# Two ResNet bottleneck blocks: the 3x3 convolution adds onto ScalarE's copies of the common product, prepares its input three combinations ahead, and forms a fourth combination by four products

## The chip, the cores and the metric

The kernel runs on one core of a Trainium2 chip. The metric is device time in microseconds (us) of one execution; a time given for a kernel is the median of its runs. A core has five engines with queues of their own: TensorE (PE in the profile; its weight loads are PEld), VectorE (DVE), ScalarE (ACT), GpSimd (POOL) and SyncE (SP), which here only issues DMAs. They meet through semaphores. TensorE writes its results to PSUM[...].

## The reference

Two bottleneck blocks in sequence over x of shape (64, 1024, 14, 14), all in fp32. Batch normalization uses the statistics of the batch itself, so each stage ends with sums over all 64 images before the next can begin.

```python
def block(x, w1, b1, g1, be1, w2, b2, g2, be2, w3, b3, g3, be3, residual_scale):
    out = relu(bn(conv(x, w1, b1, 1, 0), g1, be1))      # 1x1, 1024 -> 256
    out = relu(bn(conv(out, w2, b2, 1, 1), g2, be2))    # 3x3,  256 -> 256
    out = bn(conv(out, w3, b3, 1, 0), g3, be3)          # 1x1,  256 -> 1024
    return relu(x + softplus(residual_scale)[0] * out)

y = block(block(x, *L0), *L1)
```

## The kernel before

**Stages.** Channels lie on the 128 partitions, so 256 channels are MS = 2 slots and 1024 are CS = 8. The stages of a block follow each other: the first 1x1 convolution (`Conv1`, by a scheme of seven half-sized products for eight), the 3x3 convolution (`conv2`, L490), the Gram matrix of its output (`gram`, L798), from which the statistics of the last convolution are worked out (`conv3_stats`, L842), and the last 1x1 convolution with the residual. The last stage of block 0 is fused with the first of block 1 (`fused`, L926); block 1 ends in `final` (L900). The output of conv1, y, stays in SBUF for all 64 images, and conv2 overwrites it in place.

**The 3x3 convolution.** It runs over NG = 8 groups g of GI = 8 images. Along the rows it is a Winograd scheme of four output rows from six input rows: six combinations i = 0..5 of input rows (and of filter rows), each of which is then a convolution along a row only. They are handled in pairs, (1, 2), (3, 4), (5, 0) (`pairs`, L492). Combinations 3 and 4 have 24 lines per slot (3 rows for each of 8 images), the others 32. Along a row the columns are kept as seven odd and seven even ones, and the convolution is done with five products of filters and half lines (names at L70: D0, D1D2, D3, D1, D2), or with four for the combinations in FOUR (L67: 3, 4 and 5; names at L71: D0M2, SUM, DIFF, D3M1). One product is four fp32 matmuls, over 2 input slots and 2 output slots, of 224 columns (168 for combinations 3 and 4). Each such matmul leaves two records in the trace.

With five products, the common one (D1D2, of `sums`) belongs to the odd and the even columns alike, while D1 and D3 go to the odd columns and D2 and D0 to the even ones. With four, SUM (of `sums`) and DIFF (of `diffs`) make both halves, one by their difference and one by their sum, and D3M1 and D0M2 (of `v`, differences of neighbouring columns) are added to one half each.

**What makes and uses them.** `combine` (L516) makes the inputs of a pair: row combinations by VectorE (helper `stt`, whose line L514 shows in the profile), then in `ready` (L523) `sums` on VectorE (L531), `diffs` on GpSimd (L534), `v` on VectorE (L538) with its edge columns on ScalarE (L542, L543), and the load of the combination's filters `u` from DRAM on SyncE's queue (L547, three buffers). `products` (L590) issues the matmuls (L606 for the common products, L616 for the columns with four products, L629 for those with five), each result in one of eight PSUM banks with a common tag "ps"; ScalarE then copies the common product to SBUF (`ms`, L657 and L661). `finish` (L685) adds them on VectorE (`shared_part` L669, `column` L677), forms the output rows and writes them to y. The loop at L774 works on one pair while `combine` makes the next. Beside it ScalarE normalizes the y of the next group (`norm`, L480) and takes the moments of the group before last (`moment`, L754), whose activations of 1568 elements are the long pieces of its work.

**Filters.** `filters` (L157) makes the u of one block from the 3x3 filters, quarter by quarter (2 input slots by 2 output slots). For block 0 VectorE does it during conv1. For block 1 GpSimd does it, in four pieces beside `gram` of block 0 (`beside`, L1113: tile step 2 + 12i). A piece uses two buffers of the pool that also holds images (tag "x", four buffers in block 0); `conv3_stats` takes one more for its q (L860), and the image pairs x_0, x_1 are loaded into the same buffers after that.

**Order.** A scheduler orders each engine's instructions by readiness; matmuls that use the helper `matmul` (L155), and instructions given to `tc.keep_in_program_order`, keep their order in the program. PSUM and SBUF tiles come from pools in turn: a tile waits until the last reader of the buffer's previous content is done.

Of the kernel before, what the change touches and what calls it, by code (L numbers as in the profile page):

```python
# [33 lines left out]
FP = mybir.dt.float32  # L35
AF = mybir.ActivationFunctionType
# [26 lines left out]
BUFS = dict(u=3, t=3, r=4, sums=4, diffs=2, v=2, ms=3, f=2)  # L63
# [3 lines left out]
FOUR = 3, 4, 5  # L67
NKS = [4 if i in FOUR else 5 for i in range(NF)]
NK = max(NKS)
D0, D1D2, D3, D1, D2 = range(5)  # L70
D0M2, SUM, DIFF, D3M1 = range(4)  # L71
# [11 lines left out]
def bottlenecks(ctx: ExitStack, tc: tile.TileContext, x, w1s, w2s, w3s, pars, out):  # L83
# [73 lines left out]
    def filters(eng, b, s, o, spare):  # L157
# [24 lines left out]
        for i, (row, more, op, by) in parts.items():  # L182
# [16 lines left out]
            else:  # L199
                scaled(u[:, 0:3, :].rearrange("p k m -> p (k m)"), row, by)  # L200
                eng.tensor_tensor(
                    u[:, D1 : D2 + 1], u[:, D0 : D3 + 1 : D3 - D0], u[:, D1D2 : D1D2 + 1].to_broadcast([P, 2, P]),
                    ALU.subtract,
# [276 lines left out]
    def norm(s, y, aff):  # L480

        scale, shift = aff
        nc.scalar.activation(y, y, AF.Relu, bias=shift[:, s : s + 1], scale=scale[:, s : s + 1])
# [6 lines left out]
    def conv2(psum, pool, b, par, aff, stats):  # L490

        pairs = [(g, p) for g in range(NG) for p in ((1, 2), (3, 4), (NF - 1, 0))]  # L492
# [23 lines left out]
        def combine(g, pair, between=None):  # L516
# [4 lines left out]
            made = []  # L521

            def ready(i, r):  # L523
# [21 lines left out]
                u = pool.tile([P, MS * MS * NK * P], FP, tag="u", name="u", bufs=BUFS["u"])  # L545
                u = u[:, : MS * MS * NKS[i] * P].rearrange("p (s o k m) -> p s o k m", s=MS, o=MS, m=P)
                nc.sync.dma_start(out=u, in_=us[b][i])  # L547
                made.append((i, lines, r, sums, diffs, u))

            both = slice(0, MS)  # L550
            if pair[0] == 1:
# [11 lines left out]
                ready(1, ra)  # L563
                nc.vector.tensor_sub(rb, t1, t2)
                ready(2, rb)
            elif pair[0] == 3:
# [6 lines left out]
                ready(3, ra)  # L573
                stt(rb, t4, -2.0, t3)
                ready(4, rb)
            else:
# [7 lines left out]
                ready(NF - 1, rb)  # L584
                for s in range(MS):
                    stt(ra[:, s, 1:], rows(g, s, 0, 1, RT), 4.0, ra[:, s, 1:])
                ready(0, ra)
            return made

        def products(made, first):  # L590


            done = []
            for i, lines, r, sums, diffs, u in made:
                n = lines * WH
                four = i in FOUR

                def bank():
                    return psum.tile(2 * RT * GI * WH).rearrange("p (o n) -> p o n", o=MS)

                less = bank() if four else None
                m = bank()
                eos = [bank() for o in range(MS)]

                def shared(to, k, v, o, s):
                    nc.tensor.matmul(  # L606
                        to[:, o, :n], u[:, s, o, k], v[:, s].rearrange("p l c -> p (l c)"),
                        start=(s == 0), stop=(s == MS - 1),
                    )

                def columns(o, s, part):

                    odd, even = (eos[o][:, q, :n].rearrange("p (l c) -> p l c", c=WH) for q in range(2))
                    if four:
                        to, k, v = ((odd, D3M1, r[:, s, :, WH:]), (even, D0M2, r[:, s, :, :WH]))[part]
                        nc.tensor.matmul(to, u[:, s, o, k], v, start=(s == 0), stop=(s == MS - 1))  # L616
                        return
                    to, k, v = (
                        (odd, D1, r[:, s, :, WH:]),
                        (odd[:, :, : WH - 1], D3, r[:, s, :, WH + 1 :]),  # L620
                        (even, D2, r[:, s, :, :WH]),
                        (even[:, :, 1:], D0, r[:, s, :, : WH - 1]),
                    )[part]
                    start = s == 0 and part % 2 == 0
                    stop = s == MS - 1 and part % 2 == 1
                    if by_slot:

                        start, stop = s + part == 0, s == MS - 1 and part == 3
                    nc.tensor.matmul(to, u[:, s, o, k], v, start=start, stop=stop, skip_group_check=by_slot)  # L629

                by_slot = first and not done
                each = list(itertools.product(range(MS), range(MS)))
                if four:
                    for to, k, v in ((less, DIFF, diffs), (m, SUM, sums)):
                        for o, s in each:
                            shared(to, k, v, o, s)
                    for o in range(MS):
                        for part in range(2):
                            for s in range(MS):
                                columns(o, s, part)  # L640
                elif by_slot:
                    for s, o in each:
                        for part in range(4):
                            columns(o, s, part)
                    for o, s in each:
                        shared(m, D1D2, sums, o, s)
                else:
                    for o in range(MS):
                        for s in range(MS):
                            shared(m, D1D2, sums, o, s)  # L650
                        for part in range(4):
                            for s in range(MS):
                                columns(o, s, part)
                ms = pool.tile([P, MS, RT * GI * WH], FP, tag="ms", name="ms", bufs=BUFS["ms"])
                if i == 1:
                    for o in range(MS):
                        nc.scalar.activation(  # L657
                            ms[:, o, :n], m[:, o, :n], AF.Identity, bias=par[:, B2 + o : B2 + o + 1]
                        )
                else:  # L660
                    nc.scalar.activation(ms[:, :, :n], (less if four else m)[:, :, :n], AF.Copy)  # L661
                done.append((four, lines, m, ms, eos))
            return done

        def halves(f, lines):

            return f.rearrange("p o r (i q c) -> p o q (r i) c", i=GI, q=2)[:, :, :, :lines]

        def shared_part(item, f):  # L669

            four, lines, m, ms, eos = item
            if four:
                a, l = (v[:, :, : lines * WH].rearrange("p o (l c) -> p o l c", c=WH) for v in (m, ms))
                for q, op in enumerate((ALU.subtract, ALU.add)):
                    nc.vector.tensor_tensor(halves(f, lines)[:, :, q], a, l, op)

        def column(item, f, o):  # L677
            four, lines, m, ms, eos = item
            n = lines * WH
            to = more = halves(f, lines)[:, o]  # L680
            if not four:
                more = ms[:, o, None, :n].to_broadcast([P, 2, n]).rearrange("p q (l c) -> p q l c", c=WH)
            nc.vector.tensor_tensor(to, eos[o][:, :, :n].rearrange("p q (l c) -> p q l c", c=WH), more, ALU.add)

        def finish(g, pair, done, acc):  # L685

            fa, fb = (new("f", full if pair[0] == 3 else RT) for i in range(2))
# [482 lines left out]
```

## Time and profile before

| | |
|---|---|
| median of 3 runs | 2070.32 us (2069.67 to 2071.58) |
| the profiled execution | 2071.47 us, of which the span of its instructions is 2069.7 |
| mean granted TensorE clock | 0.987 |
| conv1 of block 0 ends on TensorE | 314.4 us |
| 3x3 stage of block 0 on TensorE | 321.4 to 618.95 us |
| head of the fused stage, TensorE idle | 745.9 to 752.2 us |
| conv1 of block 1 ends on TensorE | 1340.5 us |
| 3x3 stage of block 1 on TensorE | from 1347.4 us |

How to read it: times are us from the start of the span; engines are as named above, L12 is line 12 of the kernel, and an operand is given as partitions x elements. The page's second part shows forty slices of the span with the busy share of each engine in tenths:

```profile
PE   8999998999998989999999999899999899999998
DVE  6776559999883466777777767699989734799997
ACT  1011116224225035555555555462332330555555
POOL 0100001122218953333343333210322000566665
```

The 3x3 stages are slices 7 to 12 and 27 to 32: TensorE and VectorE are both nearly full there, ScalarE has the least to do. The peak of GpSimd at slices 13 to 15 is the filters of block 1. The largest groups of VectorE, ScalarE and GpSimd in two later groups of the 3x3 stage of block 0 (472 to 546 us) are these; the columns are line, engine, operation, output<-input, shapes, count, then busy us and mean ns of one, then the idle time before them and what ended it:

```profile
L683 DVE TENSOR_TENSOR f<-ps,ms 128x448 f32<-128x448 f32 x12 | 7.4, 616 | 3.3 <-PE ps L629 3.3
L702 DVE TENSOR_TENSOR fa<-f 128x896 f32<-128x896 f32 x2 | 4.1, 2058 | 0.0
L675 DVE TENSOR_TENSOR f<-ps,ms 128x336 f32<-128x336 f32 x8 | 3.6, 494 | 0.0
L755 ACT ACTIVATE idle<-y,center 128x1568 f32<-128x1568 f32 x9 | 14.3, 1591 | 0.0
L661 ACT ACTIVATE ms<-ps 128x448 f32<-128x448 f32 x6 | 3.3, 543 | 31.2 <-PE ps L606 31.2
L534 POOL TENSOR_TENSOR diffs<-r 128x336 f32<-128x336 f32 x5 | 17.6, 3521 | 34.1 <-DVE r L514 34.1
```

### The profile page before, as it was taken

Reading aid. Unit: us, or ns where it says so; the run is one execution under the profiler, and the core shown is the slowest. Engines: PE = TensorE matmul, PEld = TensorE weight load, DVE = VectorE, ACT = ScalarE, POOL = GpSimd, SP = SyncE. Lnnn points to the kernel's source line nnn. Section 1 sums busy time; section 2 is a strip of 40 time slices with the busy share of each in tenths; the row PEclk is TensorE's granted clock in tenths of the full one; section 3 lists DMA queues with packets and bytes.
Section 4 is the critical chain, followed back from the end, with each engine's and each line's share of the span. In section 5 each row is a group of like instructions: output and inputs, shape, how many; then the busy total and the mean of one; then the engine's idle time right before and its main releaser. Section 6 shows DMA issues by size and latency. Waiting matters only on the chain.

```text
span 2069.7 us, 27894 instructions
## 1 busy us (share of the span) xinstructions
PE 2009.1 (97%) x10120; PEld 1709.2 (83%) x10120; DVE 1572.0 (76%) x2946; ACT 809.3 (39%) x1591; POOL 657.5 (32%) x668
## 2 busy tenths in 40 slices
PE   8999998999998989999999999899999899999998
PEld 4555558999998879999999999899999898555554
DVE  6776559999883466777777767699989734799997
ACT  1011116224225035555555555462332330555555
POOL 0100001122218953333343333210322000566665
PEclk9999999999999989999999999999999999999999
DMA  7664425555533244444444444255555420589998
GB/s 285 235 240 162 184 94 191 181 206 184 199 138 125 99 190 160 183 168 176 183 160 187 160 184 172 100 197 197 194 181 206 160 92 20 222 320 339 326 340 300
DMA packets 73338, 395.33 MB, mean 191 GB/s; under 512 B 7024, under 2 KB 38000, under 8 KB 44400
## 3 DMA queue, kind: packets, MB, share of 16 engines
q1 hardware_dynamic: 63168, 324.26, 43.6%
q10 hardware_dynamic: 5904, 51.91, 6.0%
q0 software_dynamic: 4128, 17.37, 2.2%
q8 instruction: 80, 1.31, 0.3%
q14 instruction: 58, 0.48, 0.1%
HBM read 276.60 MB, written 116.92 MB: 190 GB/s over the span
## 4 chain that ended last, share of the span: by engine, by line
PE 80%; DVE 6%; POOL 6%; DMA 4%; issue 3%; ACT 1%; SPq 0%; DVEq 0%; POOLq 0%; ACTq 0%
PE ay L155 13%; PE ps L629 13%; PE cy L155 13%; PE ps L606 9%; PE ap L155 7%; PE cp L155 7%; PE ps L616 6%; PE ax L155 4%; PE cx L155 4%; POOL spare L168 2%; PE cp L810 2%; DMA x<-mid 2%; DVE x L400 2%; PE ps L155 1%; PE ap L811 1%
## 5 line engine op out<-in xcount | busy, mean ns | idle before, releaser
L274 ACT ACTIVATE cu<-cy,scale 128x196 f32<-128x196 f32 (+1 forms) x552 | 257.0, 474 | 305.8 <-PE cy L155 297.4
L534 POOL TENSOR_TENSOR diffs<-r 128x336 f32<-128x336 f32 (+1 forms) x48 | 115.5, 2408 | 651.3 <-DVE r L514 453.9
L629 PE MATMUL ps<-r,u 128*128 128x224 f32 (+1 forms) x1536 | 293.7, 343 | 13.9 <-DVE r L562 7.0
L629 PEld LDWEIGHTS ps<-r,u 128*128 128x128 f32 x1536 | 279.3, 190 | 17.8 <-issue 14.8
L400 DVE SCALAR_TENSOR_TENSOR x<-cp,scale,x 128x196 f32<-128x196 f32 (+1 forms) x368 | 178.0, 484 | 84.4 <-PE cp L155 82.3
L274 ACT ACTIVATE x<-x,shift 128x392 f32<-128x392 f32 x368 | 211.7, 614 | 68.4 <-POOL x L426 52.1
L155 PE MATMUL cy<-ct,w3s 128*128 128x196 f32 (+1 forms) x736 | 222.3, 384 | 2.5 <-ACT cu L274 2.5
L421 POOL TENSOR_TENSOR x<-x,cu 128x196 f32<-128x196 f32 (+1 forms) x184 | 167.7, 912 | 175.6 <-ACT cu L274 167.8
L155 PE MATMUL ay<-at,w1s 128*128 128x196 f32 (+1 forms) x752 | 209.3, 381 | 1.0 <-ACT au L274 1.0
L426 POOL TENSOR_TENSOR x<-x,cu 128x392 f32<-128x392 f32 x124 | 125.9, 1015 | 193.3 <-DVE x L400 188.5
L155 PEld LDWEIGHTS ay<-at,w1s 128*128 128x128 f32 x752 | 136.5, 190 | 35.4 <-ACT au L274 1.9
L155 PEld LDWEIGHTS cy<-ct,w3s 128*128 128x128 f32 x736 | 134.2, 191 | 36.8 <-ACT cu L274 4.0
L606 PE MATMUL ps<-sums,u 128*128 128x224 f32 (+1 forms) x768 | 156.0, 337 | 0.0
L447 POOL TENSOR_TENSOR x<-x,cu 128x392 f32<-128x392 f32 x120 | 125.1, 1042 | 83.4 <-DVE x L400 78.4
L274 ACT ACTIVATE au<-ay 128x196 f32<-128x196 f32 (+1 forms) x141 | 53.7, 381 | 241.7 <-PE ay L155 235.8
L661 ACT ACTIVATE ms<-ps 128x448 f32<-128x448 f32 (+1 forms) x80 | 40.4, 504 | 266.8 <-PE ps L606 266.8
L606 PEld LDWEIGHTS ps<-sums,u 128*128 128x128 f32 x768 | 133.0, 189 | 0.1
L400 DVE SCALAR_TENSOR_TENSOR x<-cx,scale,x 128x196 f32<-128x196 f32 (+1 forms) x184 | 89.1, 484 | 57.0 <-PE cx L155 51.3
L155 PE MATMUL cy<-y,w 128*128 128x196 f32 (+1 forms) x416 | 130.4, 401 | 1.1 <-DVE x L891 1.1
L616 PE MATMUL ps<-v,u 128*128 128x168 f32 (+1 forms) x768 | 131.1, 322 | 0.0
L155 PE MATMUL cx<-y,w 128*128 128x196 f32 (+1 forms) x404 | 125.9, 397 | 0.6 <-DVE x L891 0.6
L616 PEld LDWEIGHTS ps<-v,u 128*128 128x128 f32 x768 | 123.8, 188 | 0.8
(209 smaller groups left out, 4080.3 us busy)
## 6 DMA issues: line engine op xcount, KB each, us to landing
x<-in_x SPq DMA_DIRECT2D x62, 1568.0 KB, 6.6
u<-u SPq DMA_DIRECT2D x48, 1280.0 KB, 5.5
x<-mid SPq DMA_DIRECT2D x32, 1568.0 KB, 9.3
u<-u SPq DMA_DIRECT2D x48, 1024.0 KB, 4.8
mid<-x ACTq DMA_DIRECT2D x31, 1568.0 KB, 5.1
out<-x SPq DMA_DIRECT2D x124, 392.0 KB, 6.6
u<-y POOLq DMA_DIRECT2D x12, 320.0 KB, 5.7
u<-spare POOLq DMA_DIRECT2D x12, 320.0 KB, 2.5
```

The lines of the kernel that those rows point to most:

```text
L155: tc.keep_in_program_order(nc.tensor.matmul(*args, **kw))
L168: eng.tensor_scalar(to, v, by, None, ALU.mult)
L274: tc.keep_in_program_order(nc.scalar.activation(*args, **kw))
L400: nc.vector.scalar_tensor_tensor(v, bank, self.scale[:, o : o + 1], v, ALU.mult, ALU.add)
L421: nc.gpsimd.tensor_add(self.part(1, 1), self.part(1, 1), u3)
L426: nc.gpsimd.tensor_add(v, v, self.u12)
L447: nc.gpsimd.tensor_add(v, v, self.u12[:, i * self.n : (i + 1) * self.n])
L534: nc.gpsimd.tensor_sub(diffs, r[:, :, :, :WH], r[:, :, :, WH:])
L606: nc.tensor.matmul(to[:, o, :n], u[:, s, o, k], v[:, s].rearrange("p l c -> p (l c)"), start=(s == 0), stop=(s == MS - 1),)
L616: nc.tensor.matmul(to, u[:, s, o, k], v, start=(s == 0), stop=(s == MS - 1))
L629: nc.tensor.matmul(to, u[:, s, o, k], v, start=start, stop=stop, skip_group_check=by_slot)
L810: nc.tensor.matmul(g0, zt[:, c, 0:P], zt[:, c, :], start=first, stop=last)
```

## The change

**Products.** Combination 2 joins FOUR, so four of six combinations have four products. The layout of the filters changes with it: the common product's filter comes first, D0 and D3 lie next to each other, and `filters` scales a five-product combination in two instructions (D0 with D3, then D1D2) where it was one.

**Accumulation.** The PSUM banks have tags now: "l", "m", "odd" and "even", two each. A combination's common product goes to bank m, and ScalarE copies it (with the bias, for combination 1) into the combination's own odd and even banks (`start`, `biased`). The matmuls of the columns have no start flag and add to what lies there. With four products, the difference product goes to bank l and by ScalarE to SBUF (`ls`), and VectorE's one addition or subtraction per half gives the output (`outputs`); with five the banks already hold the result, and `finish` reads them straight into its sums. For the very first combination of a stage, `columns` opens the banks with a start flag, and the common product goes through `later` to `ls`. At the start of the stage four matmuls with the identity write all odd and even banks once.

**Order.** Inputs are made by a generator, one combination at a time, three ahead. The matmuls keep their order in the program: for each combination the difference product, then a part of its columns, the common product of the next combination, then the rest of its columns. The long pieces of ScalarE's work (`norm`, `moment`) go through `act`, which keeps them in program order, one after the copies of each combination (`long_work`). The load of u is split into the first product (`ua`) and the rest (`ub`), with three buffers each.

**Around it.** `conv3_stats` takes q from the pool of the Gram matrix's stage (passed as `one`) and not from the images' buffers. The pieces of filters beside `gram` start at tile step 1 + 12i.

```diff
-BUFS = dict(u=3, t=3, r=4, sums=4, diffs=2, v=2, ms=3, f=2)
+BUFS = dict(ua=3, ub=3, t=2, r=4, sums=3, diffs=4, v=3, ls=3, f=2)
-FOUR = 3, 4, 5
+FOUR = 2, 3, 4, 5
-D0, D1D2, D3, D1, D2 = range(5)
-D0M2, SUM, DIFF, D3M1 = range(4)
+D1D2, D0, D3, D1, D2 = range(5)
+SUM, DIFF, D0M2, D3M1 = range(4)
...
-                scaled(u[:, 0:3, :].rearrange("p k m -> p (k m)"), row, by)
+                row = row.rearrange("p (k m) -> p k m", k=3)
+                scaled(u[:, D0 : D3 + 1], row[:, 0::2], by)
+                scaled(u[:, D1D2], row[:, 1], by)
...
+        for tag in COLUMNS * 2:
+            n = MS * RT * GI * WH
+            matmul(psum.tile(n, tag), ident, ident[:, :1].to_broadcast([P, n]), start=True, stop=True)
...
-                u = pool.tile([P, MS * MS * NK * P], FP, tag="u", name="u", bufs=BUFS["u"])
-                nc.sync.dma_start(out=u, in_=us[b][i])
+                for tag, a, e in (("ua", 0, 1), ("ub", 1, NKS[i])):
...
+            def biased(self, to, m):
+                for v in to:
+                    if self.i == 1:
+                        for o in range(MS):
+                            nc.scalar.activation(v[:, o], m[:, o], AF.Identity, bias=par[:, B2 + o : B2 + o + 1])
+                    else:
+                        nc.scalar.activation(v, m, AF.Copy)
+            def later(self, k, v, op):
+                l = self.whole("l", k, v)
+                ls = pool.tile([P, MS * RT * GI * WH], FP, tag="ls", name="ls", bufs=BUFS["ls"])
+                self.ls, self.op = ls[:, : MS * self.n].rearrange("p (o n) -> p o n", o=MS), op
+                self.biased([self.ls], l)
+            def start(self):
+                self.ls = None
+                self.banks = {q: self.bank(COLUMNS[q]) for q in (EVEN, ODD)}
+                if not self.first:
+                    self.biased(self.banks.values(), self.whole("m", 0, self.sums))
+            def middle(self):
+                if self.four:
+                    self.later(DIFF, self.diffs, ALU.subtract)
+            def columns(self, *qs):
...
+                for q, o, (a, e, k, v), s in steps:
+                    to = self.banks[q][:, o].rearrange("p (l c) -> p l c", c=WH)[:, :, a:e]
+                    matmul(
+                        to, self.filter(s, o, k), v[:, s], start=self.first and q not in opened, stop=True,
+                        skip_group_check=True,
+                    )
+                    opened.add(q)
+                if self.first:
+                    self.later(0, self.sums, ALU.add)
...
+        def outputs(c):
+            f = new("f", c.lines // GI)
+            for q in c.banks:
+                c.add(q, half(f, q), c.column(q))
+            return f
...
+                if fa is not None:
+                    nc.vector.tensor_add(a, fa, fb)
+                    nc.vector.tensor_sub(d, fa, fb)
                 else:
+                    for q in ca.banks:
+                        nc.vector.tensor_tensor(half(a, q), ca.column(q), half(fb, q), ALU.add)
+                        nc.vector.tensor_tensor(half(d, q), ca.column(q), half(fb, q), ALU.subtract)
...
+        def long_work(g, k):
+            if g + 1 < NG and k in (1, 2):
+                norm(k - 1, y_grp[:, k - 1, g + 1], aff, act)
+                return
+            i = (0, None, None, 1, 2, 3)[k] if g + 1 < NG else k
+            if g > 1 and i < 4:
+                moment(g - 1, i // 2, i % 2)
...
+        queue = [next(made) for i in range(3)]
+        queue[0].start()
+        for k in range(NG * NF):
+            item, more = queue[0], queue[1:2]
+            item.middle()
+            qs = tuple(item.banks)
+            if item.first:
+                item.columns(*qs)
+                qs = ()
+            elif more and more[0].four:
+                item.columns(qs[0])
+                qs = qs[1:]
+            for v in more:
+                v.start()
+            long_work(*divmod(k, NF))
+            item.columns(*qs)
+            finished.send(item)
+            queue = queue[1:] + list(itertools.islice(made, 1))
...
-        q = pool.tile([P, MS, C], FP, tag="x", name="q")
+        q = one.tile([P, MS, C], FP, tag="q", name="q")
...
-            conv2(Psum(scope, ["ps"], ps=8), pool, b, pb, aff, stats2)
+            conv2(Psum(scope, ["l"], l=2, m=2, odd=2, even=2), pool, b, pb, aff, stats2)
...
-                        beside.update({2 + 12 * i: partial(piece, i // MS, i % MS) for i in range(MS * MS)})
+                        beside.update({1 + 12 * i: partial(piece, i // MS, i % MS) for i in range(MS * MS)})
```

## The prediction

> **What bounds the kernel now.** I read the page first: shares, slices, chain. Then the clock and busy time of the 3x3 stage, its waits and TensorE's timeline over one group; last the two places where TensorE stands still next to it.
>
> ```profile
> PE 2009.1 (97%) x10120; PEld 1709.2 (83%) x10120; DVE 1572.0 (76%) x2946; ACT 809.3 (39%) x1591; POOL 657.5 (32%) x668
> 361.00:398.00 37.00, 37.00 (x218) 36.78 (x217) 37.00 (x73) 5.64 (x15) 3.76 (x2) 1.00 0.54 193
> 509.00:546.00 37.00, 37.00 (x218) 36.78 (x217) 34.33 (x61) 12.15 (x26) 9.11 (x4) 1.00 0.54 193
> PE ps L629 <- DVE r L562: 7.0, 1, 7.0
> PE ps L629 <- DMA u<-u: 6.9, 1, 6.9
> ```
>
> TensorE is busy 97% of the span. The window rows give length, then busy us (instructions) of TensorE, weight loads, VectorE, ScalarE, GpSimd, then clock, DMA share, GB/s. In a group of the 3x3 convolution TensorE is busy for all 37.00 us at full clock, VectorE 37.00 in group 1 and 34.33 later, ScalarE only 12.15. The last two lines are all the waits of TensorE in the 3x3 stages (321 to 619 and 1347 to 1645): one each, at the start. So a matmul removed there is time, if VectorE and ScalarE keep up.
>
> ```profile
> 515.19 0.92 PE L606 MATMUL ps<-sums,u 128*128 128x224 f32 x4
> 515.94 3.02 PE L629 MATMUL ps<-r,u 128*128 128x224 f32 x16
> ...
> 522.41 1.30 PE L606 MATMUL ps<-diffs,u 128*128 128x168 f32 x8
> ...
> 531.61 1.67 PE L606 MATMUL ps<-diffs,u 128*128 128x224 f32 x8
> 533.12 1.68 PE L606 MATMUL ps<-sums,u 128*128 128x224 f32 x8
> 534.64 3.23 PE L616 MATMUL ps<-v,u 128*128 128x224 f32 x16
> 537.70 0.92 PE L606 MATMUL ps<-sums,u 128*128 128x224 f32 x4
> ```
>
> Starts in this timeline price a combination (each matmul leaves two records). Combination 2 with five products runs from 515.19 to 522.41: 7.22 us. Combination 5, also 32 lines but four products, from 531.61 to 537.70: 6.09. One product is 533.12 to 534.64, 1.51.
>
> ```profile
> 321.30:323.00 1.70, 1.63 (x5) 1.58 (x6) 1.60 (x3) 1.70 (x2) 0.00 (x0) 0.50 1.02 433
> 743.20 7.99 DMA x<-in_x
> 752.22 1.02 PE L155 MATMUL cp<-y,w3s 128*128 128x196 f32 x2 [6.01 <-DVE x L400]
> 755.00:758.30 3.30, 3.30 (x12) 3.30 (x12) 1.27 (x3) 1.87 (x5) 0.00 (x0) 0.50 1.01 402
> ```
>
> After each start wait the clock is 0.50 for some us. The other place is the head of the fused stage: the load of image pair 1 starts at 743.20, when GpSimd's last filter piece gives its buffer back, takes 7.99, and TensorE stands 6.01, then runs at half clock from 752.2 to 758.3.
>
> [...]
>
> **The change part by part.**
>
> (1) *Matmuls.* Combination 2 drops a product: 7.22 − 6.09 = 1.13 by these starts. Over the group (the same kind of line comes again after 36.97 us, of which combinations 3 and 4 take 4.60 each by their starts) it is 1.15 with 7.23 and 6.08; I take 1.15, times 8 groups, times 2 blocks: −18.4. In the very first combination of each block the new `columns` is called a second time with an empty tuple, and its last two lines then compute the sums product again: one more product of 1.51, twice, +3.0. It stands on TensorE's path, as nothing else delays it. Together −15.4.
>
> (2) *Additions moved from VectorE to ScalarE and TensorE.* Every combination now has its common product copied by ScalarE into both column banks (twelve copies of 448 or 336 per group), and the four-product ones get a copy of the difference product (four), for six `ms` copies before. By 543 and 450 ns that is ten more copies, some 5.2 us, plus 0.6 for the edge columns of combination 2: ScalarE goes from 12.15 to about 18 of 35.8 us. The share hides it; the question is when each copy is due. TensorE's new order puts the columns of the current combination (and the difference product of the next) between m and the columns that need its copy. The shortest cover is at combination 3's even bank: odd(2) 1.51 + difference product 1.14 = 2.65 us, against a copy of 0.45 that first needs VectorE to have read combination 1's even bank. Queued ahead of a copy on ScalarE can be one activation of 1591 ns (row L755; the normalization is as wide), since one long piece is put after each pair of copies: about 0.5 us of margin there in the worst case, more elsewhere. What waits behind a late copy is TensorE itself. Bounds: 0 to 1.6 per group. I take 0 for the steady groups and +1 for each kernel as a whole, since group 1 has VectorE at 37.00 of 37.00 and its release of banks is late there.
>
> (3) *VectorE per group.* Gone, at the rows of the groups view for two later groups: two adds of 448 in combination 1 (2 x 0.61), four of 336 in 3 and 4 (4 x 0.49), two of 448 in 5 (2 x 0.61), and in 0 four of 448 become four of 224 (−0.9). New: outputs a and d in four pieces of 448 for two of 896 (+0.3), and the edge differences of combination 2 (row of v, 0.94). About −4, from 34.3 to some 30.5 of 35.8. [...] I take no gain (nothing waits on VectorE in the steady groups) and no loss; the loss side is rival 3.
>
> (4) *Inputs three ahead, filter loads split.* The first 1/5 of u comes in 512 B pieces. The stage's DMA share is 0.54, so 48 more issues on SP and shorter pieces hide, except at the start of block 1, where u's load ends the wait: +0.4 (0 to 1).
>
> (5) *Identity matmuls at the start.* Four of 448 columns, two products' worth of the 1.51 above, so 3.0 at full clock and up to 6 at half, in the 7 us wait[...]. That clock cost 0.5 x 1.7 + 0.46 x 2.0 = 1.8 in block 0 and about 2.3 in block 1. −3 (0 to −4), since I do not know how near to the end of the wait they run.
>
> (6) *GpSimd's filters for block 1, and q.* Combination 2 becomes four-product: scaling 1.17 and subtraction 0.73 go, three of 0.46 to 0.53, one of 0.85 and two of 0.58 come: +1.6, and two split scalings add about 0.1 each: +1.8 a piece, +7 for four. GpSimd is busy without a break from 629 to 743, so its end moves to about 748, started one step (some 2.4 us) earlier. But q no longer takes one of the four x buffers, so image pairs 0 and 1 only need the third piece's buffers, given back near 719. The wait of 6.01 and 0.5 x 6.1 = 3.0 of half clock go: −9; what is late next is GpSimd's own additions, behind a piece that ends some 5 us later, in the fused stage: +2.7. I take −6.3 (−9 to 0).
>
> (7) *VectorE's filters in conv1* (block 0): the same extra work at 0.22 to 0.4 us per instruction, 0.7 us in each of four quarters; TensorE already waits 4.3 us for VectorE there: +2.5 (0 to +5).
>
> Sum: −15.4 + 1.0 + 0.4 − 3.0 − 6.3 + 2.5 = −20.8. The profiled execution took 2071.47 (span 2069.7), so 2050.7 for one like it; the median of the runs, 2070.32, lies 1.15 lower: 2049.5, rounded to 2050.
>
> **The rivals.**
>
> *R1, copies late (slower).* Place: the even bank of combinations 3 or 5, behind a 1591 ns activation or behind VectorE's release. For: each copy is now between TensorE and its next matmul, where before nothing on ScalarE was[...]. Against: the long work is placed after the copies. If one such piece stands uncovered once per group, 1.6 x 16 = 25.6 is added: 2050 + 25.6 = 2075. It decides from 20.8 / 16 = 1.3 us per group.
>
> *R2, GpSimd's longer pieces take back the gain at the fused stage.* For: GpSimd is saturated there and still ends later. Against: pairs 0 and 1 leave the chain. Part (6) becomes 0: 2050 + 6.3, about 2057.
>
> *R3, VectorE keeps the old period.* For: 37.00 of 37.00 in group 1[...]. Against: 2.7 us idle in later groups before, and 4 less work. The 18.4 goes, with 1.0 of cost: 2067.
>
> *R4, the base is not added as intended*[...]. The time would be as forecast; the same chance covers a different order of instructions than I read, such as a block start that waits longer, 2062.
>
> **How the numbers follow.** Forecast 0.58; R1 0.18; R2 0.12; R3 0.09; R4 0.03. About 0.2% (4.1 us) is what a measurement here can tell from no change: the bounds are 2066.2 and 2074.5. Faster: forecast, R2, R4 and a third of R3, 0.76. Same: the rest of R3, 0.06. Slower: R1, 0.18. Range: low end all unknown costs at their best, −15.4 − 9 − 4 = −28.4 and a little for fewer weight loads, 2040; high end 2067, which takes in R2 to R4 and leaves R1 out.
>
> **What would show it.** (1) TensorE group period 35.8 instead of 36.97, and L606-like sums written twice at each block start. (2) ScalarE at 18 of 35.8, no TensorE wait on ScalarE copies. (3) VectorE near 31[...]. (5) clock 1.00 in the first us of both 3x3 stages. (6) no 6 us wait at the fused stage. (7) TensorE waits on y in conv1 up to 7. The prediction is wrong if TensorE shows waits of a us or more for the copies in every group, or VectorE is at 100% in all of them.

## The result and the profile after

The changed kernel took 2059.07 us (four runs, 2056.76 to 2062.25), against 2070.03 for the kernel before beside it: ratio 0.9947, 95% interval 0.9929 to 0.9964, which is 7 to 15 us less. The forecast was 20 less. The profiled execution is the longest of the four, 2062.25 with a span of 2060.2, so 3.2 us above the median.

First the stage that the change is made for. From the page, the busy line; then the windows of a group of block 0 (group 1, then a later one), columns as in the prediction's window rows:

```profile
PE 2004.6 (97%) x10024; PEld 1699.7 (83%) x10024; DVE 1524.0 (74%) x2874; ACT 893.9 (43%) x1799; POOL 658.7 (32%) x708
```

```profile
361.40:397.25 35.85, 35.85 (x210) 35.62 (x210) 34.37 (x68) 13.92 (x32) 6.06 (x4) 1.00 0.59 191
509.00:544.80 35.80, 35.80 (x210) 35.58 (x209) 31.07 (x55) 20.49 (x40) 7.28 (x4) 1.00 0.59 191
```

A group takes 35.80 us where it took 36.97, and TensorE is busy for all of it, in group 1 too. VectorE fell to 31.07, ScalarE rose to 20.49, and neither shows in TensorE's waits. The waits of TensorE from the start of the first 3x3 stage to the second's, longest groups:

```profile
PE even L158 <- DVE sums L540: 5.7, 1, 5.7
PE cy L885 <- ACT y L487: 5.5, 1, 5.5
PE even L158 <- DVE r L581: 5.1, 1, 5.1
PE cy L158 <- ACT cu L278: 5.1, 2, 3.7
```

The two waits at the starts are still there, after the identity matmuls; the 6.0 us at the head of the fused stage has turned into one of 3.7 for ScalarE's `cu`. Cut at TensorE's first and last matmul of each stage, the two profiled spans compare so (lengths in us, read from the timeline). "Expected" is the prediction's own term for that stretch: part (1) and the microsecond of part (2) are given half to each 3x3 stage, part (5) in the proportion of its two costs, 1.8 to 2.3.

| stretch | before | after | change | expected |
|---|---|---|---|---|
| to the end of conv1, block 0 | 314.4 | 316.4 | +2.0 | +2.5 |
| to the first column matmul | 7.0 | 9.2 | +2.2 | 0 |
| 3x3 stage, block 0 | 297.7 | 290.9 | −6.8 | −8.5 |
| to the first Gram matmul | 6.1 | 5.5 | −0.6 | 0 |
| Gram and fused stage | 715.5 | 715.8 | +0.4 | −6.3 |
| to the first column matmul | 6.9 | 9.6 | +2.7 | +0.4 |
| 3x3 stage, block 1 | 298.3 | 290.3 | −8.0 | −8.9 |
| the rest | 424.0 | 422.6 | −1.4 | 0 |

So the 3x3 stages gave 14.8 us, and three places beside them (the two starts, and the stretch of Gram and fused stage) gave nothing or took some back. The starts, in the timeline of TensorE:

```profile
317.17 0.99 PE L158 MATMUL odd<-ident 128*128 128x448 f32 x2 [0.81 <-DVE y L329]
...
319.51 0.92 PE L158 MATMUL even<-ident 128*128 128x448 f32 x2
325.53 3.11 PE L158 MATMUL even<-r,ub 128*128 128x224 f32 x8 [5.11 <-DVE r L581]
```

and in windows of one us:

```profile
324.00:325.00 1.00, 0.00 (x0) 0.00 (x0) 1.00 (x2) 0.00 (x0) 0.00 (x0) 0.63 1.05 377
326.00:327.00 1.00, 1.00 (x4) 0.92 (x4) 1.00 (x1) 0.00 (x0) 0.95 (x1) 0.50 1.11 386
330.00:331.00 1.00, 1.00 (x5) 0.92 (x4) 1.00 (x2) 0.23 (x2) 0.19 (x1) 0.50 0.03 12
```

The identity matmuls end near 320.4. Five idle us later the columns begin, and the clock has fallen to 0.50 again: 5.5 us of the columns run at half clock, and 4.4 us in block 1 (before, 3.5 and 4.8). The DMA engines are full (1.05, 1.11) until about 328. The trace names VectorE's `r` as what ended the wait, but the first `r` was ready at 323.24. The load of the first column filters (`ub`, 1 MB) was issued at 317.78 and took 7.6 us to land, to 325.4, just ahead of the first column matmul. That load came last.

The head of the fused stage shows how a late engine passes its delay on. GpSimd, ScalarE and TensorE, one timeline each:

```profile
749.81 0.60 POOL L209 DMA_DIRECT2D u<-spare  x1 [0.30 <-POOL spare L171]
750.42 0.54 POOL L952 DMA_DIRECT2D mid<-x  x1
750.97 0.61 POOL L425 TENSOR_TENSOR x<-x,cu 128x196 f32<-128x196 f32 x1
751.52 1.98 POOL L430 TENSOR_TENSOR x<-x,cu 128x392 f32<-128x392 f32 x2
```

```profile
752.57 1.13 ACT L278 ACTIVATE x<-x,shift 128x392 f32<-128x392 f32 x2 [3.88 <-POOL x L430]
753.61 0.71 ACT L278 ACTIVATE cu<-cy,scale 128x196 f32<-128x196 f32 x2
```

```profile
744.47 0.60 PE L158 MATMUL cy<-ct,w3s 128*128 128x196 f32 x2 [1.35 <-ACT cu L278]
...
754.07 0.80 PE L158 MATMUL cy<-ct,w 128*128 128x196 f32 x2 [3.72 <-ACT cu L278]
```

GpSimd's last filter store goes out at 749.81; only then come its additions to x, on which an activation of ScalarE waits, and the copy `cu` that TensorE needs stands behind that activation. From the first Gram matmul to the last store it is 749.81 − 621.90 = 127.9 us, before it was 743.83 − 625.07 = 118.8: 9.1 us later, where 4.6 was forecast (pieces 7 longer, begun 2.4 earlier). The first filter instruction of GpSimd, before and after:

```profile
629.39 1.00 POOL L170 TENSOR_TENSOR spare<-spare 128x384 f32<-128x384 f32 x1 [8.52 <-DMA spare<-in_w]
```

```profile
626.33 1.00 POOL L173 TENSOR_TENSOR spare<-spare 128x384 f32<-128x384 f32 x1 [8.65 <-DMA spare<-in_w]
```

So the four pieces take 123.5 us instead of 114.4, 9 longer and not 7. The earlier tile step brought nothing: the first instruction waits for the load of its filters and comes 4.4 us after the first Gram matmul, before 4.3.

The row of +0.4 is made of two opposite changes. The first matmul that needs `ct` (744.47; before, 744.16) parts it in two. The first part, mostly the Gram stage, grew from 119.1 to 122.6 us, and the second, from the head of the fused stage to the end of conv1 in block 1, shrank from 596.4 to 593.3. In the first part the clock was at 0.50 for 10.4 us before and for 19.8 us after, which is enough for the 3.5 us. One such stretch after the change, in TensorE's timeline and in a window:

```profile
724.33 4.36 PE L158 MATMUL ax<-zmean,w 128*128 128x2 f32 x32
728.54 3.55 PE L158 MATMUL ax<-ones,q 128*128 128x1 f32 x16
731.96 2.96 PE L158 MATMUL cy<-y,w 128*128 128x392 f32 x4
```

```profile
728.60:732.00 3.40, 3.40 (x18) 3.40 (x17) 0.00 (x0) 0.00 (x0) 3.37 (x7) 0.50 0.95 351
```

This loss varies: e2 below, with the same program in these stages, has 13.9 us of half clock and 120.8 us in the first part, but a wait of 6.6 for `cu` and 596.2 us in the second.

### The profile page after: what moved, and what is told of

Its sections match the earlier page's. It is cut to its first block, busy times and chain, and to the rows that moved or that the text cites. A ratio compares the mean times of both kernels' runs of the same rounds, so it can differ in the third digit from the quotient of the medians.

```text
span 2060.2 us, 28080 instructions
## 1 busy us (share of the span) xinstructions
PE 2004.6 (97%) x10024; PEld 1699.7 (83%) x10024; DVE 1524.0 (74%) x2874; ACT 893.9 (43%) x1799; POOL 658.7 (32%) x708
## 4 chain that ended last, share of the span: by engine, by line
PE 82%; POOL 6%; DVE 6%; DMA 3%; issue 2%; ACT 0%; DVEq 0%; POOLq 0%; SPq 0%; ACTq 0%
PE ay L158 14%; PE cy L158 13%; PE even L158 9%; PE odd L158 9%; PE ap L158 7%; PE cp L158 6%; PE m L158 6%; PE l L158 4%; PE ax L158 4%; PE cx L158 4%; POOL spare L171 3%; PE cp L867 2%; DVE x L404 2%; PE ps L158 1%; PE ap L868 1%
## 5 line engine op out<-in xcount | busy, mean ns | idle before, releaser
L543 POOL TENSOR_TENSOR diffs<-r 128x448 f32<-128x448 f32 (+1 forms) x64 | 109.8, 1724 | 633.0 <-DVE r L525 221.0
L158 PE MATMUL m<-sums,ua 128*128 128x224 f32 (+1 forms) x752 | 145.5, 336 | 0.0
L158 PEld LDWEIGHTS m<-sums,ua 128*128 128x128 f32 x752 | 131.4, 189 | 0.2
L867 PE MATMUL cp<-zt 128*128 128x257 f32 x392 | 120.4, 389 | 4.2 <-DVE zt L887 4.2
L158 PE MATMUL cp<-y,w3s 128*128 128x196 f32 (+1 forms) x368 | 113.7, 390 | 2.4 <-DVE x L404 0.6
L158 PE MATMUL cy<-ct,w 128*128 128x196 f32 (+1 forms) x368 | 110.9, 383 | 3.7 <-ACT cu L278 3.7
L158 PE MATMUL ap<-x,w1s 128*128 128x196 f32 (+1 forms) x376 | 106.8, 388 | 6.2 <-DVE y L329 6.2
L158 PE MATMUL cp<-ct,w3s 128*128 128x196 f32 (+1 forms) x368 | 110.6, 382 | 0.0
```

Source lines behind the costliest of these rows:

```text
L158: tc.keep_in_program_order(nc.tensor.matmul(*args, **kw))
L543: nc.gpsimd.tensor_sub(diffs, r[:, :, :, :WH], r[:, :, :, WH:])
L867: nc.tensor.matmul(g0, zt[:, c, 0:P], zt[:, c, :], start=first, stop=last)
```

## The experiments

Ratios are to the kernel before, run beside each; e1 to e4 ran together, so did e5 to e8, and e9 with e10. One per mille is 2.07 us, and the changed kernel stands at 0.9947.

| run | edit | median us | ratio (95%) |
|---|---|---|---|
| e1_five | FOUR back to three | 2069.45 | 0.9995 (0.9988 to 1.0001) |
| e2_single | first common product once | 2056.32 | 0.9926 (0.9911 to 0.9941) |
| e3_whole | u in one load | 2065.64 | 0.9970 (0.9957 to 0.9983) |
| e4_last_dve | last filter piece on VectorE | 2088.81 | 1.0084 (1.0069 to 1.0099) |
| e5_warm | e2, ten identity matmuls | 2059.08 | 0.9934 (0.9922 to 0.9947) |
| e6_q_back | e2, q in the images' buffers | 2063.88 | 0.9960 (0.9947 to 0.9974) |
| e7_sp_store | e2, 18 stores on SyncE | 2047.56 | 0.9882 (0.9868 to 0.9896) |
| e8_front | e2, first filters loaded first | 2056.25 | 0.9921 (0.9906 to 0.9936) |
| e9_all | e7 with e8, eight identity matmuls | 2045.17 | 0.9867 (0.9853 to 0.9880) |
| e10_before_sp | the kernel before, 18 stores on SyncE | 2063.51 | 0.9952 (0.9938 to 0.9966) |

**e1: the fourth four-product combination.**

```diff
-FOUR = 2, 3, 4, 5
+FOUR = 3, 4, 5
...
-                c.add(q, half(f, q), c.column(q))
+                if c.ls is None:
+                    nc.scalar.activation(half(f, q), c.column(q), AF.Copy)
+                else:
+                    c.add(q, half(f, q), c.column(q))
```

> The changed kernel with combination 2 back at five products (FOUR = 3, 4, 5); where its result is needed in SBUF, ScalarE copies it. All the rest of the change stays. Theory A (the removed product is worth its full length on TensorE, all else hides): group period 36.97 again, +18.4 us in the two 3x3 stages; GpSimd's pieces get 7 us shorter, which gives back the 3.7 us wait in the fused stage and some half clock: 2059.1 + 18.4 - 4 = about 2073. Theory B (VectorE or ScalarE sets the period in some groups, so the product was partly hidden): less than +10, 2065 or below.

The period is back at 36.94 us (the same matmul at 433.18 and 470.12 in TensorE's timeline), and the two 3x3 stages are 299.5 and 298.9 us, 17.2 longer than after the change. That is theory A's term, 18.4, less some clock at the starts: 6.8 us of e1's columns ran at half clock there, against 9.9 in the changed kernel. The whole is only 10 us slower than the changed kernel, since the rest gained: the Gram and fused stage took 712.5, 3.4 less, with no wait for `cu` above the usual 1.4; the end of conv1 came 1.3 earlier, the starts waited 7.7 and 7.0. So the net is between the two theories, with A's mechanism. Without the fourth combination the new structure, as it stands, is worth nothing that these runs can tell (0.9995).

**e2: the product computed twice.**

```diff
-            item.columns(*qs)
+            if qs:
+                item.columns(*qs)
```

> The changed kernel, but the first combination of each block computes its common product once, not twice: four matmuls fewer in each block. Theory A (the second product stands on TensorE's path): -2 x 1.51 = -3.0 us, 2056. Theory B (in the first group TensorE would wait for VectorE's inputs there anyway, so the product fills a gap): 2059 within 1, and a wait of about 1.5 us appears on TensorE just after the start.

2.75 us less by the medians (4.3 by the ratios), and the 3x3 stages are 2.3 and 0.7 us shorter in the profiles; the half clock at the starts, which differs from run to run, is in these stretches too. In the changed kernel the first combination's common product stands twice in TensorE's timeline:

```profile
334.01 1.67 PE L158 MATMUL l<-sums,ua 128*128 128x224 f32 x8
335.52 1.68 PE L158 MATMUL m<-sums,ua 128*128 128x224 f32 x8
337.03 1.68 PE L158 MATMUL l<-sums,ua 128*128 128x224 f32 x8
```

In e2 the third line is gone, and the next product follows 1.51 us after the second. Theory A: the second call was on the path, and no wait took its place.

**e3: the filters in one load.**

```diff
-                for tag, a, e in (("ua", 0, 1), ("ub", 1, NKS[i])):
...
+                v = pool.tile([P, MS * MS * NK * P], FP, tag="u", name="u", bufs=BUFS["u"])
+                u = v[:, : MS * MS * NKS[i] * P].rearrange("p (s o k m) -> p s o k m", s=MS, o=MS, m=P)
+                nc.sync.dma_start(out=u, in_=us[b][i])
...
```

> The changed kernel with the filters u loaded whole again, one DMA for each combination into one of three buffers (rows of 8 to 10 KB per partition instead of pieces of 0.5 and 1.5 to 2 KB). Theory A (the start of the 3x3 stage waits for the split load, which shares the DMA engines with the five loads behind it): first matmul 6.9 to 7.0 us after the end of conv1 in both blocks instead of 9.2 and 9.6: -4.9 us, 2054. Theory B (VectorE's first r sets the start, and the load is only as late): no change, 2059. A risk of both: with one buffer per u a later load comes late and TensorE waits in the groups.

The starts did as theory A says, 6.98 and 6.91 us. But the kernel is not faster than the changed one (0.9970 against 0.9947, the intervals just overlap). The risk named is there; TensorE's waits of this run have a new line,

```profile
PE m L158 <- DMA u<-u: 4.3, 7, 1.3
```

seven waits for filters inside the groups. A likely reason: with one buffer for all of u, the load of the combination three ahead can't start before the last columns of the present one are done; in two parts the common filter's buffer comes free earlier. The 3x3 stages grew by 0.8 and 2.7 us. By itself that doesn't use up the 4.9 us won at the starts; conv1, and Gram and fused stage, were 1.2 and 1.6 longer in this profile, which this edit doesn't explain.

**e4: one filter piece on VectorE.**

```diff
-                        for _ in filters(nc.gpsimd, 1, s, o, spare):
+                        for _ in filters(nc.vector if s and o else nc.gpsimd, 1, s, o, spare):
```

> The changed kernel with the last of the four pieces of filters for block 1 made by VectorE instead of GpSimd. Theory A (GpSimd, busy with filters until 750, is what the head of the fused stage waits for): GpSimd is free some 29 us earlier, the wait of 3.7 us before the fused stage's ct product goes, and 1.5 to 2 us of half clock after it: -5, 2054. Theory B (the half clock and the small matmuls ahead of the fused stage take the gain in any case): 2059 within 1.5. Theory C (VectorE's 12 us more make zt late in the Gram stage): slower, up to 2065, with waits for zt on TensorE.

Theory C, far beyond its bound, and by another mechanism than the work that it priced at 12 us (18.6 in the trace). VectorE's waits between 640 and 700 us:

```profile
DVE spare L173 <- DMA spare<-in_w: 35.3, 1, 35.3
```

The first instruction of the piece stands in VectorE's queue for the load of its filters, which waits for buffers that GpSimd's pieces hold; `zt` is behind it, and TensorE waited 34.1 us for `zt`. Where the piece had run, the head of the fused stage showed no wait for `cu` above 1.4, as theory A has it. From the first `ct` matmul to the end of conv1 in block 1 this run took 588.5 us, against 593.3 in the changed kernel's profile and 596.2 in e2's; the whole hides that.

**e5: more identity matmuls.**

```diff
-        for tag in COLUMNS * 2:
+        for tag in COLUMNS * 5:
```

> The kernel of e2 (common product of the first combination once; 2056.3 us) with ten identity matmuls instead of four before each 3x3 stage, some 7.5 us in place of 3.1. Theory A (the array's idle time of 4 to 5 us after the identity matmuls is what halves the clock at the start): the clock stays at 1.00 over the start in both blocks: at -1.7 us for each stretch of half clock of 3.4 us, -3.4 to -5, 2052. Theory B (the clock falls anyway, or the longer row of identity matmuls holds the first matmul up): no gain, 2056 within 1, or up to +1.

Theory A came true for the clock and theory B for the time. TensorE's timeline at the start of block 0, and a window of one us there:

```profile
324.54 0.92 PE L158 MATMUL even<-ident 128*128 128x448 f32 x2
325.29 1.59 PE L158 MATMUL even<-r,ub 128*128 128x224 f32 x8
```

```profile
326.00:327.00 1.00, 1.00 (x8) 0.99 (x7) 1.00 (x2) 0.44 (x2) 0.89 (x1) 1.00 1.11 374
```

The clock is 1.00 and the same eight records that took 3.11 us take 1.59; but the columns now start 8.4 and 9.3 us after conv1 in place of e2's 7.5 and 7.8, in block 0 straight behind the tenth identity matmul, in block 1 after 0.93 us more, for `ub`. Starts and 3x3 stages together are 1.1 us shorter than in e2's profile; over the whole run nothing is gained.

**e6: q's buffer.**

```diff
-        q = one.tile([P, MS, C], FP, tag="q", name="q")
+        q = pool.tile([P, MS, C], FP, tag="x", name="q")
...
```

> The kernel of e2 with q of the statistics back in the images' buffers, as before the change. Theory A (q's buffer decides when the second image pair is loaded): its load again waits for GpSimd's last piece, now near 750, and takes 8: TensorE stands 6 to 12 us at the head of the fused stage instead of 6.6 in e2: 2058 to 2062. Theory B (GpSimd's late additions are what the head waits for, whatever the load does): 2056 within 1.

Theory A, 2 us beyond its range. The Gram and fused stage took 723.1 us (e2: 717.0), and TensorE's wait at the head reads:

```profile
754.80 1.02 PE L158 MATMUL cp<-y,w3s 128*128 128x196 f32 x2 [11.35 <-DVE x L404]
```

with VectorE waiting 10.87 us for the image pair's load just ahead of it. So the move of q does what the prediction says of it, and is worth 7 us here; it only kept the longer pieces from costing more.

**e7 and e10: GpSimd's issues.** In both kernels GpSimd issues 24 filter stores, at 605 ns each after the change (group `u<-spare`, 14.5 us in all). The edit moves those of the first three pieces to SyncE, in the changed kernel with e2's fix, and in the kernel before:

```diff
-            nc.gpsimd.dma_start(out=us[b][i][:, s, o], in_=u)
+            (nc.sync if b and not (s and o) else nc.gpsimd).dma_start(out=us[b][i][:, s, o], in_=u)
```

> The kernel of e2 with the stores of the first three filter pieces issued by SyncE and not by GpSimd, which spends 0.6 us on each of those 18 issues: GpSimd ends 10.8 us earlier, near 740. Theory A (GpSimd's end is what the head of the fused stage waits for): the wait of 6.6 us for ct falls to the 1.4 of before, and 3.4 us of half clock with it: -5 to -7, 2050. Theory B (the gain is lost to the small matmuls' half clock or to x loads): 2056 within 1.5.

> The kernel before the change with one edit only: the stores of the first three filter pieces issued by SyncE and not by GpSimd. Theory A (in the kernel before, too, GpSimd's end sets the head of the fused stage, through the second image pair's buffer): GpSimd ends 10.8 us earlier, the wait of 6.0 for that load goes, and about 3 of half clock: -6 to -9, 2062 to 2064. Theory B (the gain of e7 needs the change's q, because the load of 8 us still comes after the last piece): -1 or less, 2069 to 2071.

Theory A in both, and in e7 somewhat more than it said. In e7 GpSimd's last store is at 735.60 (in e2 at 747.39), and TensorE's timeline has no long wait at the head:

```profile
735.60 0.61 POOL L209 DMA_DIRECT2D u<-spare  x1 [0.30 <-POOL spare L171]
```

```profile
743.84 0.60 PE L158 MATMUL cy<-ct,w 128*128 128x196 f32 x2 [0.42 <-ACT cu L278]
```

The Gram and fused stage fell from 717.0 to 707.6 us, and where e2 has a clock of 0.55 and 0.60 in the windows 748 to 752 and 752 to 756 us, e7 has 1.00 throughout. In e10 it fell from 715.5 to 708.7, and the head has only the short wait that the kernel before has there as well:

```profile
744.92 0.60 PE L155 MATMUL cy<-ct,w3s 128*128 128x196 f32 x2 [1.35 <-ACT cu L274]
```

From the first `ct` matmul to the end of conv1 in block 1, e7 and e10 both take 588.5 us, as e4 does, which got there by another edit. The kernel before took 596.4, the changed one 593.3, e2 596.2. So that stretch was held by GpSimd's end in each kernel, before by way of the image load, after by way of its additions, and the hold cost 7.9 us before, 4.8 in the changed kernel's profile and 7.7 in e2's. Measured with the hold gone from both, the change with e2's fix is worth 0.9882 against 0.9952, about 14.5 us.

**e8: the first filters first.** The first combination's column filters are loaded ahead of the common ones, in two halves by input slot.

```diff
...
+                if first:
+                    loads = [(v[:, s : s + 1], w[:, s : s + 1]) for v, w in loads[1:] for s in range(MS)] + loads[:1]
...
```

> The kernel of e2, with the first combination's filters loaded as two halves by input slot, ahead of its common filters, so that the first matmuls need 512 KB and not 1280 KB of loads. Theory A (loads are served in the order of issue): the first matmul comes as early as VectorE's first r, 6.9 us after conv1's end, and 1 to 2 us are gained over both blocks: 2055. Theory B (loads issued together share the DMA engines, so the first comes late with the others): no change, start waits of 7.5 to 9, 2056.

The first matmul came 6.98 and 6.92 us after conv1, theory A; 1.4 us for both starts together, against e2's profile. The median did not show it (2056.25 against 2056.32): the 3x3 stages took as long as in e2 (578.0 against 578.2 us together), and TensorE now waits 0.6 and 1.9 us in group 1 of the two blocks, of which e9 says more. With e3, and with the landing at 325.4 above, it settles the start: the split load, with what was issued beside it, came last there.

**e9: all that helped.**

> The kernel of e7 (common product once, stores of three filter pieces on SyncE) with the order of loads of e8 and eight identity matmuls instead of four (6 us, which end before VectorE's first r is ready at 6.9). Theory A (the three places are independent): 2046 less 1.4 for the starts, less 1.7 to 3.4 of half clock at the two starts: 2041 to 2043. Theory B (what is gained at the starts is lost to a later half clock or to VectorE in the first group, as in e5): 2046 within 1.5.

2045.17 us, ratio 0.9867, the shortest of all kernels here: 8 per mille or 16.6 us below the changed kernel by the ratios. Over e7 it gained 2.4 us by the medians and 1.5 per mille by the ratios, with overlapping intervals; the median lies in theory B's range and above theory A's. In the profile the starts are at 6.98 and 6.92 and the clock stays at 1.00 behind them, but starts and 3x3 stages together are only 0.5 us shorter than in e7's. What was won at the starts is given back for the most part in group 1 of each block, where TensorE's waits have this line (360 to 400 us; the same between 1375 and 1400):

```profile
PE even L158 <- ACT even L640: 1.9, 1, 1.9
```

This is the late copy of rival R1, for which the changed kernel's own trace has no line. It shows where the columns began early or at full clock: 0.6 and 1.9 us in e8, 1.6 in block 1 of e7, 1.2 in block 0 of e5. An earlier start leaves group 1 less room. Theory B has the larger part.

## Why the prediction was right or wrong

The way and the main mechanism were right; the gain was about half of the forecast (11 us of 20.8), because parts (4), (5) and (6) did not bring what they were priced at.

- **What bounds the kernel, and part (1), matmuls: right.** 35.80 us per group, as worked out, and e1 puts the fourth combination at 17.2 us in the two stages against 18.4. The double product was seen in advance at +3.0; e2 measured 2.75 by the medians and 4.3 by the ratios.
- **Parts (2) and (3), copies and VectorE: right in effect.** No copy was late in a steady group, so R1 fell, and VectorE's 31.07 rules R3 out. ScalarE's 20.5 us was forecast as 18. The microsecond put aside for group 1 was not needed in the changed kernel, likely because its late starts left room; e9, which starts sooner, waits 1.9 us there in each block.
- **Part (4), loads: the term was mis-sized.** It gave +0.4 for the split load at block 1 and took it as hidden at block 0. It cost 2.2 and 2.7 in the profile shown (0.5 and 0.9 in e2's, so it varies); e3 and e8 make both waits 6.9 to 7.0 again. Working with the stage's mean DMA share of 0.54 was the error: at the start the share is 1.05 and 1.11 (windows 324 and 326 above), three combinations' filters are asked for at once, and the first of them lands among the others, 7.6 us after its issue. The longer block start that R4 allowed for is this one.
- **Part (5), identity matmuls: failed.** It took −3; that matmuls in the wait would keep the clock up was the author's estimate, the profile before showing only 0.50 behind each wait. It named its weak point, how near to the end of the wait they run. They run at the beginning of it, 5 us before the columns, and 9.9 us of the columns at the two starts ran at half clock, against 8.3 before. In e5 and e9, whose identity matmuls reach to the end of the wait or nearly so, all four starts ran at full clock (1.00 in e5's window and in e9's, the first eight column records in 1.59 to 1.67 us against 3.11); in e5 the filling itself then delays the start.
- **Part (6), the fused stage: the step that cost most.** −6.3 was taken, +0.4 came. The first half was right (the wait for the image pair went, from 6.0 to 0.5; e6 brings it back). The second half named what is late next, GpSimd's own additions, and priced them at 2.7. They cost 4.8 in the changed kernel's profile and 7.7 in e2's, by the 588.5 us of the runs without a hold: the pieces grew by 9 us and not 7, the earlier tile step gave none of its 2.4, and the additions hold ScalarE's queue, and with it TensorE, for 3.7 us here and 6.6 in e2. The rest is the Gram stage's 3.5 us of clock, for which the prediction had no term and which varies between runs. This is rival R2 in mechanism, with 0.12, and its 2057 was nearer than the forecast's 2050.
- **Part (7), conv1: right.** +2.0 against +2.5. TensorE's waits for y there grew from 4.3 to 5.9 us in all, and the eight records behind the longest from 4.59 to 5.09 at the half clock: most of the cost is the wait. In e1, with the old filters for combination 2, conv1 ended 1.3 earlier.

## What to carry to other kernels

When an engine's end holds the next stage, moving the buffer it gives back can move the hold to the next thing that this engine does, as here from the image load (6.0 us) to GpSimd's additions (3.7); make its work shorter. Here 18 DMA issues of 0.6 us on another queue were worth 9 us (e7 against e2), nearly the restructuring's own 11. A stage's mean DMA share (0.54 before) did not tell its first microseconds (1.05 to 1.11): there the loads of the pipeline's whole depth are asked for together, so put the first one's bytes first (6.98 and 6.92 us to the first column matmul in e8, against 7.5 and 7.8 in e2). And the cover for the clock had to reach further towards the end of the wait than in the changed kernel, without outlasting it: the four identity matmuls there, which end 5.1 and 5.7 us before the columns, left these at 0.50, e9's eight left them at 1.00, and e5's ten held block 0's up by 0.9 us against e2.

## What the runs showed of the hardware

- In the changed kernel the columns' matmuls add onto what ScalarE has put into their bank (the base of R4), and but for a stage's first combination nothing else adds the common product. In its trace ScalarE fills twelve banks a group (469 to 540.6 us), at 526 to 529 ns for 448 elements; its copies of that size to SBUF take 540. No run leaves the identity matmuls out, so whether they are needed is not shown.
- In the profile before and in that of the changed kernel every stretch of half clock, but for the one cut off by the end of the run, is 3.4, 6.8 or 10.2 us long. The prediction read the half clock behind waits. That is not the only place: in the changed kernel, ahead of the fused stage, it was at 0.50 from 727.0 to 737.3 us, and it fell while TensorE shows as busy all the time (4.20 of 4.20 us from 724.3 to 728.5, 3.40 of 3.40 in the window after it), with matmuls of two columns and then of one. The length of such stretches differs between profiles of kernels that do the same there (19.8 us in all in the changed kernel's first part, 13.9 in e2's). Half clock costs half its length: eight records take 3.11 us in it and 1.59 at 1.00, so 3.4 us of it are 1.7 us of work. The four runs of the changed kernel spread over 5.5 us.
- Sixteen starts of a 3x3 stage had four identity matmuls (the changed kernel, e1 to e4, e6 to e8). TensorE was then idle for 2.92 to 5.71 us. In the ten starts with the longest idle time, 3.44 to 5.71 us, the first columns ran at half clock in whole or in part: their first eight records took 2.34 to 3.11 us. Of the six with 2.92 to 3.33 us, three did so too (2.21 us in e8's block 0, 2.52 in e3's block 1, 3.09 in e1's block 1), and three did not (1.66 in e3's block 0 and e8's block 1, 1.67 in e7's block 1). Between 2.92 and 3.33 us the idle time alone does not tell which.
- An engine's wait for a load of its own can cost what its work never would: 35.3 us in e4 for a piece of work of 18.6 us on VectorE.
